# Pairwise bilinear products: two-tile x blocks, one PSUM ring, and some products moved to ACT and POOL

## The chip, the cores and the metric

The kernel runs on one core of one Trainium2 chip. The metric is the device time of that core in microseconds (us), the median of several executions. The engines are called PE (TensorE matmul), PEld (TensorE's loading of weights, which overlaps PE), DVE (VectorE), ACT (ScalarE), POOL (GpSimd) and SP (SyncE, which here only issues DMA transfers). All tensors are fp32.

## The reference, cut to what matters

```python
x: (4096, 32, 64)         # B samples, F fields, D
W: (496, 64, 64)          # one matrix for each pair i < j of fields
idx_i, idx_j = np.triu_indices(F, k=1)
vi = inputs[:, idx_i, :]
vj = inputs[:, idx_j, :]
vidots = jnp.einsum('bpd,pde->bpe', vi, W)
return vidots * vj        # (4096, 496, 64): 520 MB
```

The output is 520 MB, the inputs are 42 MB, and everything has to be moved once. At 432 GB/s, the best rate that the kernel before holds for a while, moving them takes 1303 us (an estimate).

## The kernel before

It takes x in 32 tiles of 128 samples, one per SBUF partition. TensorE turns pairs of fields so that the contracted dimension lies on the partitions. It multiplies field i by the matrices of its pairs, up to 16 pairs in one piece (46 pieces in a tile). VectorE multiplies each piece from PSUM by the fields x_j into an output buffer. Five groups of pieces make up a tile, and each group is stored by one DMA of about 3 MB from one of three buffers.

```python
    xpool = ctx.enter_context(tc.tile_pool(name="xpool", bufs=NX))          # NX = 3
    opool = ctx.enter_context(tc.tile_pool(name="opool", bufs=3))
    psum = ctx.enter_context(tc.tile_pool(name="psum", bufs=3, space=bass.MemoryType.PSUM))
    tpsum = ctx.enter_context(tc.tile_pool(name="tpsum", bufs=2, space=bass.MemoryType.PSUM))
    # ... cut ...
    def load_w(c: int):                       # four parts of w, one buffer
        a, b = wrows[c]
        raw[c] = rpool.tile([P, D * D], F32, tag="raw", name=f"raw_{c}")
        nc.sync.dma_start(out=raw[c][: b - a, :], in_=wflat[a:b])
    # ... cut: turn_w reorders a part, loads the next one, turns it into wT ...
    blocks = [(t, g) for g in range(len(groups)) for t in range(NX)]        # first three tiles group by group
    blocks += [(t, g) for t in range(NX, NT) for g in range(len(groups))]
    # ... cut: in the loop over all pieces ...
        nc.vector.tensor_mul(                 # every product, from PSUM
            ot[:, o : o + m, :].rearrange("p m (h e) -> p m h e", h=2),
            ps[:, :, :m, :].rearrange("p h m e -> p m h e"),
            xs[t][:, j + 1 : j + 1 + m, :].rearrange("p m (h e) -> p m h e", h=2),
        )
        if pa + m == end:
            nc.sync.dma_start(out=out[t * P : (t + 1) * P, base:end, :], in_=ot[:, : end - base, :])
            if g == len(groups) - 1 and t + NX < NT:
                load_x(t + NX, nc.scalar)
```

Of the kernel before, what the change touches and what calls it, by code (L numbers as in the profile page):

```python
# [8 lines left out]
F32 = mybir.dt.float32  # L9


@with_exitstack
def kernel(
    ctx: ExitStack,
    tc: tile.TileContext,
    x: bass.AP,
    w: bass.AP,
    out: bass.AP,
):








    nc = tc.nc

    B, F, D = x.shape  # L30
    P = 128
    assert 2 * D == P and B % P == 0
    NT = B // P
    NP = F * (F - 1) // 2
    E2 = D // 2
    BANK = 512
    CH = BANK // E2
    p0 = [i * (F - 1) - i * (i - 1) // 2 for i in range(F)]


    groups = [
        [(0, 3)],
        [(3, 5), (5, 7)],
        [(7, 9), (9, 11)],
        [(11, 14), (14, 17)],
        [(17, 20), (20, 23), (23, 26), (26, 29), (29, 31)],
    ]
    RUN = max(b - a for g in groups for a, b in g) + 1
    cap = max(p0[g[-1][1]] - p0[g[0][0]] for g in groups)

    cuts = [*range(0, NP, P), NP]
    wrows = list(zip(cuts[:-1], cuts[1:]))
    NX = 3

    const = ctx.enter_context(tc.tile_pool(name="const", bufs=1))
    rpool = ctx.enter_context(tc.tile_pool(name="rpool", bufs=1))
    ppool = ctx.enter_context(tc.tile_pool(name="ppool", bufs=2))
    xpool = ctx.enter_context(tc.tile_pool(name="xpool", bufs=NX))
    xtpool = ctx.enter_context(tc.tile_pool(name="xtpool", bufs=6))
    opool = ctx.enter_context(tc.tile_pool(name="opool", bufs=3))  # L60
    psum = ctx.enter_context(tc.tile_pool(name="psum", bufs=3, space=bass.MemoryType.PSUM))
    tpsum = ctx.enter_context(tc.tile_pool(name="tpsum", bufs=2, space=bass.MemoryType.PSUM))

    ident = const.tile([P, P], F32, tag="ident", name="ident")
    make_identity(nc, ident)

    xs = {}

    def load_x(t: int, eng):

        xs[t] = xpool.tile([P, F + 1, D], F32, tag="xs", name=f"xs_{t}")
        nc.gpsimd.memset(xs[t][:, 0, :], 0.0)  # L72
        eng.dma_start(out=xs[t][:, 1:, :], in_=x[t * P : (t + 1) * P])


    wflat = w.rearrange("p d e -> p (d e)")
    raw = {}
    wT = [
        const.tile([P, b - a, E2], F32, tag=f"w{c}", name=f"wT_{c}")
        for c, (a, b) in enumerate(wrows)  # L80
    ]
    EP = 8
    EU = BANK // P

    def load_w(c: int):
        a, b = wrows[c]
        raw[c] = rpool.tile([P, D * D], F32, tag="raw", name=f"raw_{c}")
        nc.sync.dma_start(out=raw[c][: b - a, :], in_=wflat[a:b])  # L88

    def turn_w(c: int, k: int, copy):  # L90
        r = wrows[c][1] - wrows[c][0]
        rp = ppool.tile([P, EP, 2, D], F32, tag="rp", name=f"rp_{c}_{k}")
        src = raw[c][:r, :].rearrange("p (d h e) -> p e h d", h=2, d=D)
        copy(rp[:r], src[:, k * EP : (k + 1) * EP])  # L94
        if k == E2 // EP - 1 and c + 1 < len(wrows):
            load_w(c + 1)
        for u in range(0, EP, EU):
            e0 = k * EP + u
            pt = tpsum.tile([P, EU, P], F32, tag="pt", name=f"ptw_{c}_{e0}")
            for n in range(EU):  # L100
                nc.tensor.transpose(  # L101
                    pt[:, n, :r],
                    rp[:r, u + n].rearrange("p h d -> p (h d)"),
                    ident[:r, :r],
                )
            nc.scalar.copy(  # L106
                wT[c][:, :, e0 : e0 + EU], pt[:, :, :r].rearrange("p e r -> p r e")
            )

    def turn_x(t: int, a: int, b: int):  # L110

        pt = tpsum.tile([P, RUN, P], F32, tag="pt", name=f"ptx_{t}_{a}")
        for n in range(b - a + 1):
            nc.tensor.transpose(  # L114
                pt[:, n, :],
                xs[t][:, a + n : a + n + 2, :].rearrange("p f d -> p (f d)"),
                ident,
            )
        xT = xtpool.tile([P, RUN, P], F32, tag="xT", name=f"xT_{t}_{a}")
        nc.scalar.copy(xT[:, : b - a + 1, :], pt[:, : b - a + 1, :])  # L120
        return xT

    load_x(0, nc.scalar)
    load_w(0)
    for t in range(1, NX):
        load_x(t, nc.sync)


    blocks = [(t, g) for g in range(len(groups)) for t in range(NX)]
    blocks += [(t, g) for t in range(NX, NT) for g in range(len(groups))]  # L130
    steps = [
        (t, g, r, i, c0, min(CH, F - 1 - i - c0))
        for t, g in blocks
        for r in groups[g]
        for i in range(*r)
        for c0 in range(0, F - 1 - i, CH)
    ]


    AHEAD = 6  # L140
    due: dict = {}
    seen = set()
    for s, (t, g, r, i, c0, m) in enumerate(steps):
        if (t, r) not in seen:
            seen.add((t, r))
            due.setdefault(max(0, s - AHEAD), []).append(("x", t, r))
        for c, (a, b) in enumerate(wrows):
            if c and a < p0[i] + c0 + m and c not in seen:
                seen.add(c)
                for k in range(E2 // EP):  # L150
                    due.setdefault(s - 18 + 4 * k, []).append(("w", c, k))

    engines = [nc.vector.tensor_copy, nc.gpsimd.tensor_copy, nc.scalar.copy, nc.vector.tensor_copy]
    for k in range(E2 // EP):
        turn_w(0, k, engines[k])

    xT = {}
    ot = None
    for s, (t, g, r, i, c0, m) in enumerate(steps):
        for what, *args in due.get(s, ()):  # L160
            if what == "x":
                tt, rr = args
                xT[tt, rr] = turn_x(tt, *rr)
            else:
                turn_w(*args, nc.gpsimd.tensor_copy)

        base, end = p0[groups[g][0][0]], p0[groups[g][-1][1]]
        pa = p0[i] + c0
        if pa == base:
            ot = opool.tile([P, cap, D], F32, tag="ot", name=f"ot_{t}_{g}")  # L170
        ps = psum.tile([P, 2, CH, E2], F32, tag="ps", name=f"ps_{s}")
        for c, (a, b) in enumerate(wrows):
            lo, hi = max(pa, a), min(pa + m, b)
            if lo < hi:
                for h in range(2):
                    rows = slice(h * D, (h + 1) * D)
                    nc.tensor.matmul(  # L177
                        ps[:, h, lo - pa : hi - pa, :],
                        xT[t, r][rows, i - r[0] + 1 - h, :],
                        wT[c][rows, lo - a : hi - a, :],  # L180
                        start=True,
                        stop=True,
                    )
        o = pa - base
        j = i + 1 + c0
        nc.vector.tensor_mul(  # L186
            ot[:, o : o + m, :].rearrange("p m (h e) -> p m h e", h=2),
            ps[:, :, :m, :].rearrange("p h m e -> p m h e"),
            xs[t][:, j + 1 : j + 1 + m, :].rearrange("p m (h e) -> p m h e", h=2),
        )  # L190
        if pa + m == end:
            nc.sync.dma_start(
                out=out[t * P : (t + 1) * P, base:end, :],
                in_=ot[:, : end - base, :],
            )
            if g == len(groups) - 1 and t + NX < NT:
                load_x(t + NX, nc.scalar)


# [25 lines left out]
```

## Time and profile before

| | before |
|---|---|
| median of 3 runs | 1371.99 us (1371.41 to 1372.5) |
| bytes moved | 562.97 MB |
| one tile in the middle | 41.4 us |
| first store issued | 35.48 us |

The head of the profile page gives the span and, for each engine, the busy time, its share of the span and the number of instructions. The fourth part gives the chain of work that ended last, as shares of the span by engine.

```profile
span 1370.6 us, 18821 instructions
...
PE 1292.4 (94%) x7776; PEld 675.2 (49%) x7776; DVE 1183.4 (86%) x1474; ACT 227.5 (17%) x418; POOL 31.4 (2%) x51
...
PE 50%; DMA 32%; DVE 16%; issue 1%; POOL 0%; DVEq 0%; POOLq 0%; SPq 0%
```

The chain runs through PE for half of the span, and PE is busy for 94% of it.

### The profile page before, as it was taken

To read this page: it belongs to the slowest core of one execution; us is meant where nothing else is said; L and a number is where in the kernel's file an instruction comes from. 1 tells how busy PE (TensorE), PEld (TensorE's weight loads), DVE (VectorE), ACT (ScalarE), POOL (GpSimd) and SP (SyncE) were. 2 spreads that over 40 slices of the span, in tenths; PEclk is the share of its full clock that TensorE was granted. 3 is DMA by queue.
4 is the path that set the end of the run, shared out by engine and by line. 5 is a ranking of instruction groups with operands and counts; after the bars stand their busy time and mean duration, and the time that the engine had idled before them with its cause. 6 is when DMAs were issued, how large, how long until landed. Compare 5 with 4: busy or idle time off the path is not lost.

```text
span 1370.6 us, 18821 instructions
## 1 busy us (share of the span) xinstructions
PE 1292.4 (94%) x7776; PEld 675.2 (49%) x7776; DVE 1183.4 (86%) x1474; ACT 227.5 (17%) x418; POOL 31.4 (2%) x51
## 2 busy tenths in 40 slices
PE   5999999999999999999999999999999999999995
PEld 3555554444554445544445554455544445544553
DVE  2888899888889888989889889899898889898995
ACT  2222211111111111111111111111111111111110
POOL 2220000000000000000000000000000000000000
PEclk9999999999999999999999999999999999999998
DMA  5999999999999999999999999999999999999998
GB/s 214 382 406 405 410 430 432 431 424 419 410 422 428 414 416 421 414 425 419 415 421 414 419 425 423 416 397 426 424 423 418 410 416 418 422 427 417 421 404 354
DMA packets 28292, 562.97 MB, mean 411 GB/s; under 512 B 3136, under 2 KB 3136, under 8 KB 3136
## 3 DMA queue, kind: packets, MB, share of 16 engines
q1 hardware_dynamic: 23888, 530.33, 91.8%
q10 hardware_dynamic: 4320, 31.46, 5.5%
q8 instruction: 61, 1.00, 0.3%
q14 instruction: 23, 0.19, 0.0%
HBM read 41.68 MB, written 520.09 MB: 410 GB/s over the span
## 4 chain that ended last, share of the span: by engine, by line
PE 50%; DMA 32%; DVE 16%; issue 1%; POOL 0%; DVEq 0%; POOLq 0%; SPq 0%
PE ps L177 38%; DMA out_dram<-ot 31%; DVE ot L186 16%; PE ptx L114 10%; DMA raw<-in_L_rec_W_dram 1%; PE ptw L101 1%; DVE rp L94 0%; POOL rp L94 0%; DVEq L186 0%; POOLq L94 0%; SPq L88 0%; DVEq L94 0%
## 5 line engine op out<-in xcount | busy, mean ns | idle before, releaser
L186 DVE TENSOR_TENSOR ot<-ps,xs 128x1024 f32<-128x1024 f32 (+7 forms) x1472 | 1181.3, 868 | 157.7 <-PE ps L177 99.8
L177 PE MATMUL ps<-wT,xT 64*128 64x512 f32 (+13 forms) x6272 | 1090.8, 467 | 46.9 <-DVE ot L186 44.5
L177 PEld LDWEIGHTS ps<-wT,xT 64*128 64x128 f32 x6272 | 515.4, 186 | 509.3 <-DVE ot L186 302.0
L120 ACT COPY xT<-ptx 128x512 f32<-128x512 f32 (+1 forms) x384 | 207.5, 541 | 1088.7 <-PE ptx L114 1086.3
L114 PE MATMUL ptx<-ident,xs 128*128 128x128 f32 x1376 | 240.9, 290 | 0.2 <-ACT wT L106 0.2
L114 PEld LDWEIGHTS ptx<-ident,xs 128*128 128x128 f32 x1376 | 144.5, 141 | 145.6 <-issue 138.5
L101 PE MATMUL ptw<-ident,rp 128*128 128x128 f32 (+1 forms) x128 | 20.5, 304 | 16.6 <-DVE rp L94 12.5
L72 POOL MEMSET xs<- 128x64 f32 x32 | 4.8, 151 | 1130.5 <-DVE ot L186 1090.8
L101 PEld LDWEIGHTS ptw<-ident,rp 128*128 128x128 f32 (+1 forms) x128 | 15.6, 156 | 26.0 <-issue 16.1
L94 POOL COPY rp<-raw 128x1024 f32<-128x1024 f32 (+1 forms) x13 | 26.0, 2018 | 74.0 <-DMA raw<-in_L_rec_W_dram 32.1
L106 ACT COPY wT<-ptw 128x512 f32<-128x512 f32 (+1 forms) x32 | 17.4, 574 | 35.7 <-PE ptw L101 35.7
L94 DVE COPY rp<-raw 128x1024 f32<-128x1024 f32 x2 | 2.1, 1026 | 15.4 <-DMA raw<-in_L_rec_W_dram 11.4
L94 ACT COPY rp<-raw 128x1024 f32<-128x1024 f32 x1 | 1.9, 1945 | 0.0
L106 ACT ACT_TABLE_LOAD x1 | 1.3, 1283 | 1.2 <-PEq L212 1.2
masks.py:199 POOL TENSOR_SCALAR_AFFINE_SELECT ident<-ident 128x128 f32<-128x128 f32 x1 | 0.3, 292 | 0.0
masks.py:197 POOL MEMSET ident<- 128x128 f32 x1 | 0.2, 204 | 0.3 <-POOLq L212 0.3
L212 POOL MEMSET const-float32-0.0<- 128x1 f32 x1 | 0.1, 99 | 0.2 <-issue 0.2
L212 POOL MEMSET const-bfloat16-1.0<- 128x1 bf16 x1 | 0.1, 102 | 0.0
L212 POOL MEMSET const-uint8-127<- 128x1 uint8 x1 | 0.1, 102 | 0.0
L212 POOL MEMSET const-float32-1.0<- 128x1 f32 x1 | 0.1, 99 | 0.0
## 6 DMA issues: line engine op xcount, KB each, us to landing
out_dram<-ot SPq DMA_DIRECT2D x64, 3360.0 KB, 15.5
out_dram<-ot SPq DMA_DIRECT2D x64, 2880.0 KB, 15.7
out_dram<-ot SPq DMA_DIRECT2D x32, 3392.0 KB, 16.8
xs<-in_r_inputs_dram ACTq DMA_DIRECT2D x30, 1024.0 KB, 14.5
raw<-in_L_rec_W_dram SPq DMA_DIRECT2D x3, 2048.0 KB, 10.6
xs<-in_r_inputs_dram SPq DMA_DIRECT2D x2, 1024.0 KB, 13.6
raw<-in_L_rec_W_dram SPq DMA_DIRECT2D x1, 1792.0 KB, 10.4
```

The source lines that it names most:

```text
L72: nc.gpsimd.memset(xs[t][:, 0, :], 0.0)
L94: copy(rp[:r], src[:, k * EP : (k + 1) * EP])
L101: nc.tensor.transpose(pt[:, n, :r], rp[:r, u + n].rearrange("p h d -> p (h d)"), ident[:r, :r],)
L106: nc.scalar.copy(wT[c][:, :, e0 : e0 + EU], pt[:, :, :r].rearrange("p e r -> p r e"))
L114: nc.tensor.transpose(pt[:, n, :], xs[t][:, a + n : a + n + 2, :].rearrange("p f d -> p (f d)"), ident,)
L120: nc.scalar.copy(xT[:, : b - a + 1, :], pt[:, : b - a + 1, :])
L177: nc.tensor.matmul(ps[:, h, lo - pa : hi - pa, :], xT[t, r][rows, i - r[0] + 1 - h, :], wT[c][rows, lo - a : hi - a, :], start=True, stop= ...
L186: nc.vector.tensor_mul(ot[:, o : o + m, :].rearrange("p m (h e) -> p m h e", h=2), ps[:, :, :m, :].rearrange("p h m e -> p m h e"), xs[t][ ...
L212: nc = _bacc.Bacc("TRN2", target_bir_lowering=False, num_devices=1)
```

## The change

The intent is to free the compute engines, so that the DMA alone sets the pace, and to start the output earlier. x comes in blocks of two tiles by one load. Eight fields are turned at once into one 1024-element PSUM tile. One PSUM ring of four serves everything. Seven of the 46 products of a tile go through an ACT copy and a POOL multiplication. The parts of w are loaded at once into buffers that are not needed yet.

```diff
+    NB = 2
-    psum = ctx.enter_context(tc.tile_pool(name="psum", bufs=3, space=bass.MemoryType.PSUM))
-    tpsum = ctx.enter_context(tc.tile_pool(name="tpsum", bufs=2, space=bass.MemoryType.PSUM))
+    psum = ctx.enter_context(tc.tile_pool(name="psum", bufs=4, space=bass.MemoryType.PSUM))
+    aside = (1, 3, 5, 7, 9, 11, 13)
 ... cut: x loads of 2 tiles, "(p k) f d -> p (k f) d" ...
-        raw[c] = rpool.tile([P, D * D], F32, tag="raw", name=f"raw_{c}")
+        pool, tag = ((opool, "ot"), (xpool, "xs"), (const, "w3"), (xpool, "xs"))[c]
+        raw[c] = pool.tile([P, D * D], F32, tag=tag, name=f"raw_{c}")
 ... cut: turn_x of RUN = 8 fields; all 4 parts of w turned within the first tile ...
+    load_w(0)
+    load_w(1)
+    load_x(0, nc.sync, 1, NB)
+    load_w(2)
 ... cut ...
+        if i in aside and c0 == 0:
+            tmp = tpool.tile([P, CH, 2, E2], F32, tag="tmp", name=f"tmp_{s}")
+            nc.scalar.copy(tmp, src)
+            nc.gpsimd.tensor_mul(dst, tmp, xj)
+        else:
+            nc.vector.tensor_mul(dst, src, xj)
-                out=out[t * P : (t + 1) * P, base:end, :],
+                out=rows_of(out, blk).rearrange("(p k) n d -> p k n d", k=NB)[:, kt, base:end, :],
```

The order also changes. The kernel before made the first three tiles group by group, so it needed each part of w late. The changed one goes tile by tile from the start.

## The prediction

> **What bounds the kernel now.** I began with the page's slices, which show each engine and the DMA over forty equal stretches (34.3 us each):
>
> ```profile
> PE   5999999999999999999999999999999999999995
> DVE  2888899888889888989889889899898889898995
> DMA  5999999999999999999999999999999999999998
> GB/s 214 382 406 405 410 430 432 431 424 419 410 422 428 414 416 421 414 425 419 415 421 414 419 425 423 416 397 426 424 423 418 410 416 418 422 427 417 421 404 354
> DMA packets 28292, 562.97 MB, mean 411 GB/s; under 512 B 3136, under 2 KB 3136, under 8 KB 3136
> ```
>
> Three things are near full at once: TensorE, VectorE and the DMA. "9" does not tell a full pipe from a nearly full one, but the last row does: slices six to eight reach 430 to 432 GB/s, and later ones mostly 414 to 425. So the pipe has a few per cent left in the long middle, and half of the first slice is empty. I then asked for stretches (columns: stretch, length, busy us of PE, PEld, DVE, ACT, POOL, granted clock, DMA share, GB/s):
>
> ```profile
> 160.00:200.00 40.00, 39.56 (x244) 20.70 (x243) 36.87 (x46) 6.49 (x12) 0.15 (x1) 1.00 1.01 433
> 242.42:283.80 41.38, 39.64 (x241) 20.43 (x239) 36.87 (x46) 6.49 (x12) 0.15 (x1) 1.00 1.01 431
> 325.20:366.60 41.40, 39.09 (x233) 20.57 (x230) 36.83 (x45) 6.01 (x11) 0.00 (x0) 0.96 0.98 412
> 1030.32:1071.71 41.39, 39.61 (x241) 20.42 (x239) 36.88 (x46) 6.49 (x12) 0.15 (x1) 1.00 0.99 418
> 0.00:41.40 41.40, 24.37 (x110) 14.83 (x112) 12.20 (x12) 11.80 (x18) 11.40 (x14) 0.92 0.59 231
> ```
>
> One tile of 128 rows takes 41.39 us in the middle and asks for 17.3 MB (16.25 written, 1.05 read): 418 GB/s. At the 432 GB/s that the same kernel holds for 100 us while a backlog of output is queued, 17.3 MB need 40.05 us. The compute side thus sets the 41.39 us, with TensorE busy for 39.6 of it, and the DMA is only 1.3 us behind. The waits show how the three hand over (engine, what it waited for, total us, times, longest):
>
> ```profile
> PEld ps L177 <- DVE ot L186: 302.0, 594, 2.7
> ...
> DVE ot L186 <- PE ps L177: 99.8, 150, 5.5
> DVE ot L186 <- DMA out_dram<-ot: 50.1, 48, 2.3
> PE ps L177 <- DVE ot L186: 44.5, 86, 1.8
> ```
>
> VectorE waits now for products, now for a free output buffer; TensorE waits for a PSUM slot. No single engine is the bound. The start is different (time order: start, length, engine, operation):
>
> ```profile
> 25.85 3.77 POOL L94 COPY rp<-raw 128x1024 f32<-128x1024 f32 x2 [11.67 <-DMA raw<-in_L_rec_W_dram]
> ...
> 35.48 0.35 SPq L192 DMA_DIRECT2D out_dram<-ot  x1
> ```
>
> The single raw buffer makes w's second part load late; POOL reorders it at 25.85 us, TensorE's queue stands behind it, and the first output is issued only at 35.48. The trace's packets show the pipe empty from about 15 to 18.5 and 25 to 36.5 us.
>
> **The skill against this trace.** "DMA: Bandwidth & Descriptors", section "Where 436 GB/s comes from", puts the fabric's ceiling at 435 GB/s. The trace agrees: a 23,040-byte output packet takes 855 ns in the median, 26.9 GB/s on each of 16 engines, 431 together. The same page's 358 GB/s per core is not seen here: 411 is the mean. "GPSIMD Engine Reference", section 3.1, gives 4497 ns for a two-input fp32 operation on 2048 elements; half, about 2.25 us, is my estimate for a 1024-element product. The trace has only POOL copies (2.0 us for 1024), which fits. "SBUF — State Buffer", section "Who interferes with whom", says that a VectorE instruction with one SBUF input does not contend with GpSimd. A product reads PSUM and SBUF, so I expect none; the trace has too little POOL work to show it. "TensorE: Matmul & The Clock Gate", section on HAM oscillation, warns of idle gaps over about 3.4 us. Two dips to half clock of 3.4 us each, at 344 and 883 us, are in the clock record; the stretch above with 0.96 holds the first, and its DMA fell to 412.
>
> **The change, part by part, per tile of 128 rows.** Durations are from these groups (line, engine, operation, tiles, count, total us, mean ns of one):
>
> ```profile
> L186 DVE TENSOR_TENSOR ot<-ps,xs 128x1024 f32<-128x1024 f32 x512 | 623.5, 1218 | 132.7 <-PE ps L177 81.8 <-DMA out_dram<-ot 50.1
> ...
> L114 PE MATMUL ptx<-ident,xs 128*128 128x128 f32 x1376 | 240.9, 290 | 0.2 <-ACT wT L106 0.2
> ...
> L120 ACT COPY xT<-ptx 128x512 f32<-128x512 f32 x224 | 131.0, 585 | 618.8 <-PE ptx L114 616.4 <-PE ps L177 2.4
> ...
> L120 ACT COPY xT<-ptx 128x384 f32<-128x384 f32 x160 | 76.5, 478 | 469.9 <-PE ptx L114 469.9
> ```
>
> *Turning x:* 1376/32 = 43 transposes become 32. In time order four take 0.66 us, 0.165 each, so TensorE saves 11 x 0.165 = 1.8 us. Twelve ACT copies (6.5 us) become four of 1024 elements. The two sizes above give 0.84 ns an element plus 155 ns, so 1.01 us each, 4.0 in all.
>
> *Products moved:* seven of 1024 elements leave VectorE. Its six products in a row for the first group (5760 elements) took 6.49 us, so one of 1024 is 1.15: VectorE goes from 36.9 to about 28.8 us. ACT gets 7 x 1.01 = 7.1, in all 11. POOL gets 7 x 2.25 = 16. Both are far below 40, and no moved product is the last of its output group.
>
> *One PSUM ring of four:* TensorE may run one step further ahead, so some of the 302 + 44 us of waiting for VectorE (10.8 per tile, overlapping) goes. TensorE at 39.6 - 1.8 = 37.8 us, less what its modelled ends contain of waiting, no longer needs 40.
>
> *Loads and stores:* bytes are unchanged. The x packets become 16 KB in place of 8 KB, which at 7 ns a packet (from 309 ns for 8,192 and 611 for 16,384 bytes) is under 1 us in total. Outputs keep their packet sizes but go to every second row.
>
> So after the start the DMA alone sets the pace: about 40.1 to 40.3 us per tile instead of 41.39.
>
> *The start:* x's first half and three of w's four parts (8.4 MB with x's second half) are queued at once and keep the pipe full until about 22 us: 19.4 us of data plus 2 to 3 us of slow first packets, as w's first ones show (1.2 to 1.5 us instead of 0.61). w's first part still lands near 11.4 us, and four pieces turned take the first matmul to about 19 (21.5 before). The first group needs 90/496 of about 30 us of matmuls, 5.4, and three w turns at 1.15, then one product: issue near 30, data from 31.5. That leaves some 9 us empty, against about 15. But all of w is now turned within one tile, not three: TensorE has about 48 us of work there, and I count 4 us more of gaps and slow w reads before it stops mattering.
>
> *The sum.* 562.97 MB at 432 GB/s are 1303 us. Add 2 before the first byte, 3 slow first reads, 9 empty before the first output, 4 in the rest of the first tile, 3 for slow w reads beside output (those packets averaged 790 to 940 ns), 4 for small losses over 31 tiles, and 4.4 between the last packets and the end (1366.2 to 1370.6 before) plus 1 in the drain: 1333. The timed median is 1.4 us above the profiled span: about 1335. I put the point a little higher because the surprises are on that side: 1337.
>
> **Rivals.** (1) *Reads and writes disturb each other.* w's 16 KB packets beside output took up to 940 ns where 611 is clean. The x packets now have that size; if all 2048 lost 190 ns, 2048 x 190/16 = 24 us come back and the time is about 1358. Against it: in the backlogged stretches the 8 KB x packets cost nothing (432 GB/s with the x load in it), and they alternate with output on another queue, as these will. (2) *The compute side stays the bound:* ACT stands in the PSUM ring twice, for turns and moved products, and each x load makes it wait for POOL's memset. If a tile still took 41 us, the gain would be the start alone, about 8 us: 1364. Against it: the largest engine sum is 37.8. (3) *Clock dips:* TensorE will idle more while it waits for the DMA, so half-clock windows may come more often. One such window costs about 1.7 us of a tile with some 3 to 5 us of slack and two queued outputs, so I give it under 5 us: 1340. (4) *The row stride of the stores doubles to 248 KiB* and HBM might serve it worse; nothing in the trace speaks to it, and 3% slower packets would undo everything, 1372.
>
> **Range and chances.** The floor of this plan is near 1325: nothing lost after the start. Rivals 1 and 2 in part reach 1358. The 2% line is 1344.6 us, 8 above my point. I give 0.70 for faster, 0.29 within, 0.01 slower.
>
> **What would show it.** Right: middle slices at 429 to 433 GB/s; VectorE near 29 us a tile and waiting mostly for the output DMA; first output issued near 30 us. Wrong: x or output packets longer than 611 and 855 ns in the median (rivals 1, 4); GB/s near 418 with TensorE waiting for ACT (rival 2); the first output not earlier than 35 us.

## The result, and the profile after

| | before | after |
|---|---|---|
| median, same rounds | 1371.70 us (1370.6 to 1372.5) | 1359.86 us (1359.48 to 1364.98) |
| profiled span | 1370.6 | 1357.5 |
| first store issued | 35.48 | 29.97 |

The ratio is 0.9923, with a 95% interval of 0.9898 to 0.9947. A ratio is the mean time of one kernel's fast runs over that of the other's fast runs of the same rounds, so it is not quite the ratio of the medians. The kernel became 0.8% faster, which is inside the 2% that counts as the same. The predicted 1337 us was 23 us too low, and the measured time lies just above 1358, up to which the prediction's range reached. Its likeliest outcome, faster by more than 2% (0.70), did not come.

The same slices of the page for the changed kernel, each now 33.9 us long (PEclk is the granted TensorE clock in tenths):

```profile
PE   5998988888888888988889888899888889888894
...
DVE  5686876767677676766667767677776777767783
...
PEclk9998998989999999998989999999898999999997
DMA  7999999999999999999999999999999999999997
GB/s 291 388 430 431 426 424 431 431 422 426 401 424 413 430 423 412 428 409 431 410 417 425 413 433 407 421 423 410 428 412 424 426 409 424 406 431 428 417 419 335
```

VectorE has fallen to 6 or 7 tenths, and TensorE has holes. Only the DMA row is full. Yet the GB/s row is half of what the prediction named as a sign of being wrong: near 418. The other half, TensorE waiting for ACT, did not come (3.2 us in all). In slices three to nine the flow lies between 422 and 431, and from there on it swings between 401 and 433. A freed compute side did not raise the flow. The groups (line, engine, operation, tiles, count, total us, mean ns of one, idle time before them) confirm the durations:

```profile
L209 DVE TENSOR_TENSOR ot<-ps,xs 128x1024 f32<-128x1024 f32 (+15 forms) x1248 | 938.6, 807 | 378.4 <-DMA out_dram<-ot 195.3
...
L207 POOL TENSOR_TENSOR ot<-tmp,xs 128x1024 f32<-128x1024 f32 x224 | 527.3, 2360 | 623.5 <-ACT tmp L206 397.7
L206 ACT COPY tmp<-ps 128x1024 f32<-128x1024 f32 x224 | 226.7, 1012 | 465.5 <-PE ps L192 460.6
```

That mean of 807 ns mixes shapes; the 1024-element products alone are this group:

```profile
L209 DVE TENSOR_TENSOR ot<-ps,xs 128x1024 f32<-128x1024 f32 x288 | 351.1, 1219 | 80.4 <-PE ps L192 79.6
```

The waits (engine, what it waited for, total us, times, longest):

```profile
DVE ot L209 <- DMA out_dram<-ot: 195.3, 97, 5.2
POOL ot L207 <- DMA out_dram<-ot: 169.5, 73, 5.6
DVE ot L209 <- PE ps L192: 156.9, 212, 2.7
```

VectorE's wait for a free output buffer was 50.1 us before, and it is 195.3 us now. The compute side is ahead and waits for the DMA, as the change intended. The chain agrees, where the DMA had 32% before and PE 50%:

```profile
DMA 50%; PE 23%; DVE 18%; POOL 4%; issue 3%; ACT 0%; DVEq 0%; SPq 0%; POOLq 0%; ACTq 0%
```

The time line shows when x is loaded, once every two tiles, and so the pace (start, length, engine):

```profile
602.75 0.34 ACTq L75 DMA_DIRECT2D xs<-in_r_inputs_dram  x1
685.94 0.34 ACTq L75 DMA_DIRECT2D xs<-in_r_inputs_dram  x1
767.97 0.34 ACTq L75 DMA_DIRECT2D xs<-in_r_inputs_dram  x1
```

Two tiles took 83.19 and 82.03 us, a mean of 41.3 us per tile. **The pace of the steady part hardly changed**: by the packet records used below, two tiles took 82.94 us before and 82.72 after. Nearly all of the gain lies in the first 170 us. In the first 41.4 us the kernel now moves 300 GB/s, where it moved 231:

```profile
0.00:41.40 41.40, 27.47 (x168) 17.86 (x168) 22.18 (x20) 15.25 (x15) 18.72 (x15) 1.00 0.76 300
```

In slices one to five the kernel before is 333 GB/s below 430 in sum (214, 382, 406, 405, 410); at 34.3 us a slice and 430 GB/s that is 26.5 us of transfers not made. The changed one is 184 below (291, 388, 430, 431, 426), which is 14.5 us. The difference is 12 of the 13 us by which the span fell.

**What holds the DMA at 41.4 us.** The printed views average over sixteen DMA engines. I therefore went to the records of single packets in the trace, of which no view exists; the numbers from here to the end of the section are my own sums of them. A packet without disturbance takes 855 ns (23,040 bytes), 996 (26,880), 1006 (27,136) or 611 (16,384, x). Each engine moves eight packets of each store, so two tiles without disturbance are 2 x 8 x (0.855 + 1.006 + 0.855 + 0.996 + 0.996) + 8 x 0.611 = 80.2 us, with the small completion packets 80.3. That is 40.15 us per tile, close to the prediction's 40.05.

But the sixteen engines do not finish a store together. In the steady part fifteen end within 1 to 2 us of each other, and one ends 5 to 6 us after their median. I followed that last engine packet by packet over 15 of the 16 stores of four tiles (each engine's eight data packets, the completion packet and those of x). Each packet starts when the one before it ends: the gap is zero within the 0.02 us of a store that the records resolve. It is never idle, and its packets are longer: 879 ns in the mean instead of 855, 1029 instead of 996, 1046 instead of 1006. Two tiles take it 82.7 us. Followed further, from 305 to 1341 us, it stays the same engine through 127 stores with 0.5 us of gaps in all. Of its output packets there 5% are undisturbed; of the other fifteen engines' it is 66%. There are three output buffers and a store frees its buffer only when its last packet has landed, so the fifteen others soon wait for this one.

The lag of the last engine behind the median of the others, read at the second store of a tile, shows when this begins. It is 1.7 us at 98 us, 2.8 at 180, 4.4 at 263 and 6.5 at 346 us, and it stays between 4.7 and 6 from there. While the lag grows, the core shows 422 to 431 GB/s. When the buffers are used up, all engines go at the pace of the slowest. The kernel before does the same (1.2 us at 190 us, 5.1 at 356, then 3.5 to 5.1). Its lagging engine is hardly ever idle either: from 562 to 985 us, through 52 stores, its gaps are 0.1 us in all.

### The profile page after: what moved, and what is told of

Its sections match the earlier page's. It is cut to its first block, busy times and chain, and to the rows that moved or that the text cites. A ratio compares the mean times of both kernels' runs of the same rounds, so it can differ in the third digit from the quotient of the medians.

```text
span 1357.5 us, 17867 instructions
## 1 busy us (share of the span) xinstructions
PE 1171.5 (86%) x7424; PEld 681.2 (50%) x7424; DVE 951.3 (70%) x1259; ACT 371.1 (27%) x367; POOL 546.2 (40%) x253
## 4 chain that ended last, share of the span: by engine, by line
DMA 50%; PE 23%; DVE 18%; POOL 4%; issue 3%; ACT 0%; DVEq 0%; SPq 0%; POOLq 0%; ACTq 0%
DMA out_dram<-ot 49%; PE ps L192 19%; DVE ot L209 18%; PE ptx L113 4%; POOL ot L207 3%; DMA raw<-in_L_rec_W_dram 1%; POOL rp L94 1%; PE ptw L103 0%; ACT tmp L206 0%; DVE rp L94 0%; DVEq L209 0%; DVE xT L117 0%; ACT wT L106 0%; SPq L211 0%; POOLq L207 0%
## 5 line engine op out<-in xcount | busy, mean ns | idle before, releaser
L209 DVE TENSOR_TENSOR ot<-ps,xs 128x1024 f32<-128x1024 f32 (+15 forms) x1248 | 938.6, 807 | 378.4 <-DMA out_dram<-ot 195.3
L192 PE MATMUL ps<-wT,xT 64*128 64x512 f32 (+14 forms) x6272 | 1025.2, 467 | 118.0 <-DVE ot L209 105.5
L192 PEld LDWEIGHTS ps<-wT,xT 64*128 64x128 f32 x6272 | 554.0, 193 | 554.6 <-DVE ot L209 281.9
L207 POOL TENSOR_TENSOR ot<-tmp,xs 128x1024 f32<-128x1024 f32 x224 | 527.3, 2360 | 623.5 <-ACT tmp L206 397.7
L206 ACT COPY tmp<-ps 128x1024 f32<-128x1024 f32 x224 | 226.7, 1012 | 465.5 <-PE ps L192 460.6
L117 ACT COPY xT<-ptx 128x1024 f32<-128x1024 f32 x127 | 128.5, 1012 | 470.2 <-PE ptx L113 470.2
L113 PE MATMUL ptx<-ident,xs 128*128 128x128 f32 x1024 | 143.8, 285 | 48.9 <-DVE ot L209 34.3
L113 PEld LDWEIGHTS ptx<-ident,xs 128*128 128x128 f32 x1024 | 113.2, 144 | 95.4 <-issue 51.3
L106 ACT COPY wT<-ptw 128x1024 f32<-128x1024 f32 (+1 forms) x15 | 14.7, 984 | 28.1 <-PE ptw L103 28.1
L94 DVE COPY rp<-raw 128x1024 f32<-128x1024 f32 (+1 forms) x9 | 11.0, 1233 | 12.3 <-DMA raw<-in_L_rec_W_dram 11.9
```

The costliest lines, as they stand in the source:

```text
L94: copy(rp[:r], src[:, k * EU : (k + 1) * EU])
L106: copy(wT[c][:, :, k * EU : (k + 1) * EU], pt[:, :, :r].rearrange("p e r -> p r e"))
L113: nc.tensor.transpose(pt[:, n, :], xs[blk][:, s : s + 2, :].rearrange("p f d -> p (f d)"), ident)
L117: copy(xT, pt)
L192: nc.tensor.matmul(ps[:, h, lo - pa : hi - pa, :], xT[blk, kt, n // RUN][h * D : (h + 1) * D, n % RUN, :], wT[c][h * D : (h + 1) * D, lo - ...
L206: nc.scalar.copy(tmp, src)
```

## The experiments

Fourteen kernels ran, all in three timed rounds and, where nothing else is said, with correct results. "Two tiles" is the time from one store of the lagging engine to the same store two tiles on, averaged over ten such pairs (tiles 6 to 26), again my own reading of packet records. Square brackets after a time hold the 95% interval of its ratio to the kernel before. "A" in the expectations is the theory that TensorE's instruction stream stretches the packets of the lagging engine; up to halves and onepass it has the form that this engine also fetches TensorE's instructions. "B" is a rival that differs from run to run.

| kernel | PE and PEld instructions | two tiles, us | median, us | ratio to before |
|---|---|---|---|---|
| no_pe (wrong) | 0 | 81.05 | 1323.12 | 0.9652 |
| best | 8,576 | 81.78 | 1348.95 | 0.9843 |
| onepass | 8,576 | 81.84 | 1347.39 | 0.9826 |
| all_dve | 14,848 | 82.66 | 1357.49 | 0.9903 |
| after | 14,848 | 82.72 | 1359.86 | 0.9923 |
| thin_pe (wrong) | 14,848 | 82.74 | 1360.36 | 0.9924 |
| before | 15,552 | 82.94 | 1371.70 | 1 |
| halves | 22,272 | 83.73 | 1380.45 | 1.0058 |
| pool_tied | 14,848, and 5,888 more on POOL | 84.15 | 1379.55 | 1.0069 |

### Does the compute side or the DMA hold the pace: no_pe and thin_pe

no_pe takes all of TensorE's work away, and ACT's and POOL's part of the products with it. It keeps every load and store, through three fixed output buffers; its outputs are wrong.

```diff
-                        nc.tensor.matmul( ... )      # and all transposes
+        nc.vector.tensor_mul(dst[:, :1], xj[:, :1], xj[:, :1])
```

> Wrong result on purpose: the changed kernel's loads and stores, all 160 of the same size and order through the same three output buffers, but no TensorE work and one small VectorE product per step. Theory A (one DMA engine is the bound, because it also carries TensorE's instruction blocks of 16 KB, 58 of them at about 0.65 us, which is 38 us): without TensorE's instructions no engine lags, and the time is about 1318 us, with middle slices at 430 to 434 GB/s. Rival B (the compute chain through PSUM, half-clock windows and three buffers sets the pace): about 1318 us too. Rival C (stores to every second row, or stores at all, can't be served faster than now): about 1350 us.

thin_pe keeps all of TensorE's work but lets VectorE multiply only one pair of each piece, and ACT and POOL none; its outputs are wrong too. (Both cuts leave out the fixed buffers.)

```diff
-        if i in aside and c0 == 0:
-            ... ACT copy, POOL product ...
-        else:
-            nc.vector.tensor_mul(dst, src, xj)
+        nc.vector.tensor_mul(dst[:, :1], src[:, :1], xj[:, :1])
```

> Wrong result on purpose: the changed kernel with its whole TensorE stream, the turns, and the same loads and stores, but each product writes one pair in place of up to 16, so VectorE, ACT and POOL have little to do. Theory A: TensorE's instruction blocks are all there, so the time stays within 6 us of the changed kernel, 1352 to 1364 us, and one DMA engine ends several us after the other fifteen. Rival B: with VectorE nearly free TensorE needs under 36 us a tile, the compute chain is out of the way, and the time falls to 1318 to 1330 us.

no_pe took 1323.12 us [ratio 0.9638 to 0.9666] and thin_pe 1360.36 [0.9909 to 0.9939]. First the busy row and the GB/s row of no_pe, then the busy row of thin_pe:

```profile
DVE 242.8 (18%) x1484; POOL 24.8 (2%) x29
...
GB/s 373 416 430 434 434 426 434 427 433 430 426 430 428 431 431 428 432 427 431 431 426 434 424 432 429 428 431 429 431 428 431 432 423 431 426 435 428 433 434 310
```

```profile
PE 1143.2 (84%) x7424; PEld 706.0 (52%) x7424; DVE 324.0 (24%) x1485; ACT 144.6 (11%) x143; POOL 27.7 (2%) x30
```

no_pe holds 423 to 435 GB/s from the third slice to the last but one, so the same transfers can go nearly at the predicted pace. Its expectation missed one thing: an engine lags here too, by up to 8.1 us at the end. But it lags in another way: 96% of its output packets are undisturbed, and a few are very long (25 of 853, from 291 to 1156 us, by more than 12%). thin_pe has VectorE at 24%, so it cannot be late, and it still needs 41.4 us per tile. That takes VectorE, ACT and POOL off the list: with TensorE's stream in the program the pace is 41.4, without it 40.5. no_pe alone could not show this, as both of its theories expected the same time. The pair does not yet tell TensorE's duration (84% busy) from its instructions.

### Whether one engine's share of the bytes can be lightened: split120

Every fourth tile's first group was stored as 120 and 8 partitions.

```diff
+            for a0, b0 in (((0, 120), (120, P)) if g == 0 and t % 4 == 2 else ((0, P),)):
+                nc.sync.dma_start(out=dst_rows[a0:b0, kt, base:end, :], in_=ot[a0:b0, : end - base, :])
```

> Right result: in every fourth tile the first output group is stored in two parts, partitions 0 to 119 and 120 to 127. If a store of 120 rows runs on the 15 lowest DMA engines and one of 8 rows on the 8 lowest, the highest engine is relieved of 8 x 8 packets of 855 ns, 55 us, and the lowest eight get 8 x 0.86, 7 us. Theory A if the lagging engine is the highest one: 1325 to 1335 us. Theory A if it is one of the lowest eight: about 7 us longer, 1366. If it is in between: no change, 1358 to 1361. Rival B: no change or slightly longer.

It took 1437.85 us (1410 to 1457), and its profile fell in the slow state. Its two fast runs, 1429 and 1410 us, already make it slower than the kernel before, by 3.6% [1.0275 to 1.0438]. The issue lines (KB of each, us from issue to landing) of the slow profile show where to look:

```profile
out_dram<-ot SPq DMA_DIRECT2D x64, 3360.0 KB, 15.2
...
out_dram<-ot SPq DMA_DIRECT2D x8, 2700.0 KB, 31.6
```

A store of 120 partitions takes twice as long as a larger one of 128, and 566 of the 1,024 packets of 23,040 bytes in the split groups took more than 1.5 us instead of 0.855. Why splitting makes packets slow is not shown, and no fast profile of it exists. The question of which engine lags stays open; nothing in the records names an engine.

### Are the moved products worth anything: all_dve

```diff
-    aside = (1, 3, 5, 7, 9, 11, 13)
+    aside = ()
```

> Right result: the changed kernel with no product moved to ACT and POOL, so VectorE has all 46 per tile, some 36.9 us, again. Theory A: the pace of 41.3 us a tile is not VectorE's, so within 4 us of the changed kernel. Rival B: VectorE and TensorE wait for each other more, and at least half of the 12 us gained is lost: 1366 us or more.

It took 1357.49 us [0.9889 to 0.9918], 2.4 us less than the changed kernel. VectorE is back at 88%, and the pace does not change (82.66 us for two tiles):

```profile
PE 1189.6 (88%) x7424; PEld 674.8 (50%) x7424; DVE 1189.2 (88%) x1483; ACT 144.6 (11%) x143; POOL 17.7 (1%) x29
```

The moved products, the largest part of the change, earn nothing, because VectorE was not what the kernel waited for.

### More and fewer TensorE instructions: halves and onepass

halves issues each matmul of more than eight pairs as two. It has the same columns and results, and half as many TensorE instructions again.

```diff
+                    mid = lo + 8 if hi - lo > 8 else hi
+                    for u0, u1 in ((lo, mid), (mid, hi)):
+                        if u0 < u1:
                             nc.tensor.matmul( ... u0, u1 ... )
```

> Right result: the changed kernel with every matmul of more than eight pairs issued as two. The same columns go through TensorE, but its program grows from 14,887 to 22,311 instructions, from 58 to 87 blocks of 16 KB. Theory A (one DMA engine carries these blocks besides its sixteenth of the data and sets the pace): 29 blocks at about 0.65 us more, so 1358 + 19 = 1377 us, give or take 5. Rival B (the compute chain): TensorE has some 4 us of slack a tile, so 1358 to 1364 us.

onepass declares the turned x and w as float32r, so that each product takes one matmul in the trace and not two (3,136 in place of 6,272). The data type is not exact fp32, which a user must be free to accept; the outputs passed the comparison with the reference.

```diff
-        xT = xtpool.tile([P, RUN, P], F32, tag="xT", ...)
+        xT = xtpool.tile([P, RUN, P], mybir.dt.float32r, tag="xT", ...)
-            wT[c] = const.tile([P, r, E2], F32, tag=f"w{c}", ...)
+            wT[c] = const.tile([P, r, E2], mybir.dt.float32r, tag=f"w{c}", ...)
```

> Products in the one-pass form of fp32 (operands rounded by the copies that write them), so the result may miss the tolerance; that is not the point. TensorE's program shrinks from 14,887 to 8,615 instructions, from 58 to 33.7 blocks, and the matmuls take less time. Theory A: 24.5 blocks less at 0.65 us, 1343 us, give or take 5. Rival B: TensorE is far from busy and the compute chain is gone: 1320 to 1330 us.

halves took 1380.45 us [1.0034 to 1.0082], inside the expected 1377 give or take 5. (Its profile is of the fastest run, 1374.98 us; the other three took 1380.4 to 1381.0, and why is not known.) onepass took 1347.39 [0.9809 to 0.9842], also close to A. That A's numbers came true does not show its fetching; what speaks against that stands under "What stays open". The busy row of halves, then the busy and clock rows of onepass:

```profile
PE 1206.3 (88%) x11136; PEld 1081.3 (79%) x11136; DVE 953.2 (69%) x1259; ACT 371.3 (27%) x367; POOL 546.1 (40%) x253
```

```profile
PE 960.1 (71%) x4288; PEld 630.4 (47%) x4288; DVE 946.7 (70%) x1259; ACT 370.8 (28%) x367; POOL 548.8 (41%) x253
...
PEclk9755555555555555555655555565555555555555
```

halves hardly changes PE's busy time (88% against 86%), and PE still waits; onepass runs at half the granted clock for nearly all of the time and is faster. So neither TensorE's busy time nor its clock is what counts. The time follows the number of instructions. (What grows along with it, the weight loads' time for one, 681 to 1081 us in halves, these two runs don't separate.) Between onepass, after and halves two tiles rise by 0.88 us for 6,272 instructions and by 1.01 us for 7,424: 0.140 and 0.136 us per thousand, a straight line. no_pe lies 0.4 us above that line carried to zero (82.72 - 14.848 x 0.138 = 80.67). The lagging engine's own packets show the same order. Those of 23,040 bytes take 874 ns in the mean in onepass (468 to 729 us), 883 in the changed kernel, 892 in halves and 900 in pool_tied, the last experiment below, and in none of the stretches that could be followed (260 to 1035 us long) is that engine idle for more than 0.7 us in all.

### Smaller stores: fine

Nine groups and five output buffers in place of five and three. If a late engine only costs at the end of each store, more and smaller buffers help.

```diff
-    groups = [(0, 3), (3, 7), (7, 11), (11, 17), (17, F - 1)]
+    groups = [(0, 2), (2, 4), (4, 6), (6, 8), (8, 11), (11, 14), (14, 18), (18, 23), (23, F - 1)]
-    opool = ... bufs=3
+    opool = ... bufs=5
```

> Right result: nine output groups per tile with five buffers in place of five with three, in the same space. Theory A: the lagging engine stays as busy as before and only the first store comes earlier, so 1352 to 1359 us. Rival B (three buffers too few to cover a slow group): the stores never run dry and the time falls to 1325 to 1340 us.

It took 1370.87 us [0.9975 to 1.0019], slower than the changed kernel: rival B falls, and A's number missed as well. A tile took 41.63 us, by packets. Four more stores of eight packets per engine at 7 ns each (the constant part of the packet times) are 0.22 us a tile, or 7 us in all. That is an estimate which accounts for most of the miss; I did not test it apart.

### The start: late_w and late_w2

late_w loads w's later parts only when the part before has been reordered, as before the change.

```diff
     load_w(0)
-    load_w(1)
     load_x(0, nc.sync, 1, NB)
-    load_w(2)
+    # load_w(1) after the last order_w(0, .), load_w(c + 1) after the last turn_w(c, .)
```

> Right result: the changed kernel with w's parts loaded one after the other again, each when the one before has been reordered. Theory A says that all of the gain of 12 us lies before the stream of stores is full, so most of it goes: 1366 to 1373 us. If the gain came from the steady part, 1358 to 1362.

It took 1361.63 us [0.9915 to 0.9944], which lies in the second range but tells little. The loads of the second and third parts were issued within the first 3 us all the same. Their buffers were free, and SyncE issues a load as soon as nothing that it has to wait for stands before it. The edit thus changed almost nothing. late_w2 has the same order of loads and puts the first three parts through one buffer, which makes the loads serial.

```diff
-        pool, tag = ((opool, "ot"), (xpool, "xs"), (const, "w3"), (xpool, "xs"))[c]
+        pool, tag = ((const, "w3"), (const, "w3"), (const, "w3"), (xpool, "xs"))[c]
```

> The changed kernel with w's four parts loaded one after the other through one buffer (the fourth through x's), each when the part before has been reordered, as in the kernel before; late_w did not make them serial. If the gain of 12 us is the start (first store 5.5 us earlier, and fewer holes in the traffic before the stream of stores is full): most of it goes, 1364 to 1371, with an unchanged pace of 41.4 us per tile afterwards. If early w loads earn nothing because only the time of the first store counts: 1358 to 1363.

It took 1385.59 us [1.0095 to 1.0126], 26 us more than the changed kernel, at an unchanged pace of 82.73 us for two tiles. The direction was right and the size far off. The time line of SyncE's queue (start, length, operation) shows why:

```profile
1.64 16.55 SPq L88 DMA_DIRECT2D raw<-in_L_rec_W_dram  x2
40.36 0.35 SPq L211 DMA_DIRECT2D out_dram<-ot  x1
40.80 0.38 SPq L88 DMA_DIRECT2D raw<-in_L_rec_W_dram  x1
66.30 56.64 SPq L211 DMA_DIRECT2D out_dram<-ot  x8
```

The first store is issued at 40.36 us, and the second waits until 66.30, since the first tile needs all of w. The kernel before hid its late loads behind the first group of three tiles. The new order of tiles and the early loads therefore belong together: the start's gain is a net of two large terms, and the early loads are worth 26 us to this order.

### Both helpful edits: best and best2

best is all_dve with the float32r of onepass.

> All products on VectorE (2.4 us better than the changed kernel) together with one-pass fp32 in TensorE (12.5 us better). If the two act on different things: 1359.9 - 2.4 - 12.5 = 1345. If what all_dve gained was the same thing (fewer instructions and waits in all): 1347, as onepass alone. Expected 1345, range 1343 to 1348, so 1.9% faster than the kernel before. Not exact fp32: products are rounded more, the outputs must still agree with the reference.

It took 1348.95 us [0.9828 to 0.9858], no better than onepass alone. Its pace was a little better (81.78), but its first store's packets began at 30.5 us where onepass's began at 27.0. I took this for VectorE's doing, as it makes the first tile alone there, and best2 gives the helpers back in the first tile only:

```diff
-        if i in aside and c0 == 0:
+        if i in aside and c0 == 0 and t == 0:
```

> onepass, with ACT and POOL helping in the first tile only. best missed its 1345: its pace was 40.88 us per tile (onepass 40.91) but its first store began 3.5 us later (30.5 instead of 27.0), by our reading since VectorE alone makes the first tile. If that reading is right: onepass's start and best's pace, 1347.4 - 0.03*31 = 1346.5 (1345.5 to 1347.5). If the helpers were worth more than the start, 1347.5 to 1349.

It took 1348.59 us (1346.87 to 1349.72) [0.9830 to 0.9862]. In its profile the first store began at 27.1 us and the span was 1345.1, against 1346.8 for best and 1345.5 for onepass. The start moved as expected, but the timed runs do not separate the three. The reading of the cause was also too quick. In best the first store was issued only 0.9 us later than in onepass (27.11 instead of 26.19 us). But the fourth part of w was issued at 23.0 us, before it, and its packets held the queue until 30.5 and beyond, where onepass and best2 issue it just after the store. So most of the delay was that load's. onepass, best and best2 all beat both kernels by more than their intervals, by 0.8 to 1.0% against the changed one (the ratio of their ratios, as they ran in other rounds) and by 1.5 to 1.7% against the one before, at the price of exact fp32.

### Any engine's instructions, or TensorE's alone: pool_instr, pool_paced, pool_tied

all_dve with four tiny POOL instructions after each of the 1,472 pieces.

```diff
+        for n in range(4):
+            nc.gpsimd.memset(dot[:, n : n + 1], 0.0)
```

> The changed kernel with all 46 products on VectorE, and four one-column memsets by POOL after each of the 1,472 pieces: 5,888 more instructions on an engine that is otherwise idle; TensorE, VectorE and the transfers as in all_dve (1357.5 us). Theory A1, any engine's instruction stream stretches the packets of the lagging DMA engine: from halves and no_pe some 0.060 us per tile and thousand instructions, so 0.35 us per tile and 1357.5 + 11 = 1368.5 (1365 to 1372). Theory A2, TensorE's stream alone does (by its place, or because it has two instructions, weight load and matmul, for each step): 1355 to 1360. Rival C, POOL's work slows VectorE[...]: shows as longer tensor_mul durations than in all_dve.

It took 1414.53 us [1.0305 to 1.0340] and settled nothing. The memsets depend on nothing, so POOL ran them all in the first 270 us, ahead of its share of turning w. The steady part, without them, was as in all_dve (82.67 us for two tiles). pool_paced made one of the four wait for the piece.

```diff
+        nc.gpsimd.tensor_copy(dot[:, 0:1], ot[:, o, 0:1])
+        for n in range(1, 4):
+            nc.gpsimd.memset(dot[:, n : n + 1], 0.0)
```

> pool_instr ran all its memsets in the first 250 us, ahead of POOL's share of the start, so it said nothing of the pace. Here POOL's four one-column instructions per piece follow VectorE's product of that piece (the first copies one column of it), so 184 of them run in each tile, 5,888 in all; else as all_dve (1357.5 us, 41.32 us per tile). Theory A1, any engine's instructions count: slope 0.060 us per tile and thousand instructions from no_pe and halves, so 41.32 + 0.35 = 41.68 us per tile and 1357.5 + 11 = 1369 (1365 to 1373). Theory A2, TensorE's alone count: 41.3 to 41.4 us per tile and 1356 to 1361. If VectorE's products get longer or POOL becomes late (releasers of the stores), the run decides nothing.

It took 1489.10 us [1.0851 to 1.0888], for the same reason: the three memsets still ran ahead. One copy per piece was left in the steady part, and two tiles took 83.20 us instead of 82.66. So pool_tied lets the memsets write the copy's column, which keeps their order.

```diff
+        nc.gpsimd.tensor_copy(dot[:, 0:1], ot[:, o, 0:1])
+        for n in range(3):
+            nc.gpsimd.memset(dot[:, 0:1], 0.0)
```

> In pool_paced the memsets ran ahead again, and only one small copy per piece (92 in two tiles) was left for the steady part, where two tiles took 83.10 us instead of all_dve's 82.57. Here the three memsets write the same column as the copy, so all four follow the product: 368 POOL instructions in two tiles. What costs: by the bytes of their fetch (pool_paced's 5,888 more instructions added 57 blocks of 8 KB, so 3.6 more blocks in two tiles, 309 ns each at the pace of a clean 8 KB packet): 83.7 us in two tiles and 1357.5 + 18 = 1375; by the number of instructions at TensorE's slope (0.12 us in two tiles and thousand of the program): 83.3 and 1369; by what each tied POOL instruction cost in pool_paced (0.53 us for 92): 84.7 and 1391; nothing, if POOL's instructions don't count: 82.6 and 1357.5.

It took 1379.55 us [1.0054 to 1.0084], 22 us more than all_dve. The start was as in all_dve (first store at 32.3 us against 32.8), and two tiles took 84.15 us, 1.49 more, for 368 more POOL instructions. The slices of POOL and the GB/s row:

```profile
POOL 4654555545455454554545555455554545545553
...
GB/s 319 390 427 431 434 418 421 397 425 416 401 411 403 432 412 411 409 404 421 410 421 412 404 417 416 413 405 409 421 396 425 417 403 412 410 423 411 418 413 321
```

POOL's instructions are now spread evenly, and the flow falls from the seventh slice on. VectorE's products kept their 869 ns, so this is not a slower VectorE. The cost is 4.0 ns per POOL instruction. TensorE's slope in the same unit is 2.2 ns: 0.138 us in two tiles for a thousand of the program, of which a sixteenth (62) falls in two tiles. The expectation by bytes of instructions (83.7 us, 1375) came nearest and was too low. So TensorE is not special: instructions of an engine that is otherwise idle cost the lagging DMA engine time as well. The lagging engine's chain has no gap of more than 0.03 us from 307 to 1280 us, so this is not a wait for POOL. One limit remains: the copies wait for VectorE's product and all four follow one another, and the run does not separate that from their being fetched.

## Why the prediction was wrong

**The step that failed** is this one: "So after the start the DMA alone sets the pace: about 40.1 to 40.3 us per tile instead of 41.39." Its first half held, its figure did not. The DMA alone does set the pace, but at 41.36 us, and it had set it before too, at 41.47. "The compute side thus sets the 41.39 us" was wrong. The 40.05 us came from "the 432 GB/s that the same kernel holds for 100 us while a backlog of output is queued". Those 100 us were a transient: fifteen engines running ahead of the sixteenth until the three output buffers were used up.

**The mis-sized term** of the sum is "4 for small losses over 31 tiles". What stands in its place is the stretch of the lagging engine: 82.72 - 80.3 = 2.4 us in two tiles, some 37 us over 31. The sum with measured terms closes. Undisturbed packets give 1307 us for each engine (the median time of each size, with the completion and instruction packets that the prediction's 1303 leaves out). What undisturbed packets do not fill of the first 41.4 us is 12.7 us (the prediction's 2, 3 and 9 make 14). With the 37 this is 1357, against a last packet at 1356. The separate terms for the rest of the first tile and for slow w reads, 7 us, are then not needed. Nor was the term of 4.4 us "between the last packets and the end" what it was taken for. In the kernel before, fifteen engines had ended by 1366.3 us, and the last one's data ended at 1369.05. That was the lagging engine, in plain sight before the prediction was made.

**"No single engine is the bound"** was wrong of the kernel before, since one DMA engine was. The mean over sixteen engines, 418 GB/s, hid it. VectorE waited only 50 us for the DMA, most likely because TensorE and VectorE took just about as long as the lagging engine. When they were freed, the wait grew to 195 us and the time per tile stayed.

**The start was right, and better than predicted.** Of the 35 us that the prediction hoped for, the 12 that came are the start's, for which it had counted about 8. The first matmul began at 20.03 us (19 predicted), and the first store was issued at 29.97 ("near 30"). One reading was loose: the parts of w that came beside output before took 789 and 898 ns a packet in the mean (some over 1400), not "790 to 940". **The durations were right:** a POOL product took 2360 ns (2.25 us predicted), a 1024-element ACT copy 1012 ns (1.01), and VectorE was busy for 951.3 / 32 = 29.7 us a tile (28.8). The Trainium skill's "GPSIMD Engine Reference" was a good source for POOL. The expected absence of contention between VectorE and POOL also held: a 1024-element product took 1219 ns after and 1218 before. Since VectorE was not the bound, none of this bought time.

**The rivals.** Rival 1 (slow x packets) fell: their median is 611 ns. Rival 4 (the row stride) fell: output packets kept their 855, 996 and 1006 ns. That rival 1 had named nearly the right time (1358) is luck. Rival 2 came near too (1364), for a wrong cause, as all_dve and thin_pe show. Rival 3 (the clock) was common and harmless: there are 21 half-clock windows of 3.4 or 6.8 us, and onepass is faster with the clock at half for nearly all of its time. A fifth rival was missing: that sixteen engines which share one store need not finish together.

**What stays open.** Shown are that the lagging engine is hardly ever idle in the followed stores, that its packets are stretched, and that the stretch grows in a line with TensorE's instructions and also with POOL's. Not shown is how. The Trainium skill, "Runtime: NRT & Kernel Launch", section "Instruction fetch mechanics", says that instructions come by DMA in blocks of 16 KiB, 256 each, at a cost that is "mostly hidden". The count fits: 14,848 / 256 = 58 blocks, and the page of the changed kernel has this line:

```profile
q8 instruction: 58, 0.95, 0.3%
```

The size does not rule it out. 58 / 16 blocks in two tiles are 2.2 us at the 611 ns of an undisturbed packet of that size, and 3.4 us at the 935 ns that they took in the median, if all of them fell on one engine; the stretch is 2.4. These products are estimates. The placing speaks against it. None of the 45 blocks between 305 and 1341 us lies among the lagging engine's packets, and those are stretched nearly all by a little, only two of 1,011 output packets by more than 12%. So fetching on that very engine is not the way there, and how instructions slow it stays open. One rival was not tested: each timed run has a span and a granted clock, so a profiler was recording in all of them, and a cost of recording each instruction would look the same.

## What to carry to other kernels

Before calling a stream of stores "almost bound by the DMA", look at when each engine finishes a store and not only at the mean rate, and do not take the rate of the first 300 us for the lasting one: here, with three buffers, the slowest DMA engine set the pace only after its lag had used them up. Test the bound by emptying an engine (thin_pe, no_pe) before moving work off it. When the DMA is full, fewer instructions may be worth more than shorter ones: here a thousand TensorE instructions cost 2 to 3 us (onepass, the changed kernel and halves).

## What the Trainium skill lacked or had wrong

- "Runtime: NRT & Kernel Launch", section "Instruction fetch mechanics", calls the cost of fetching "mostly hidden". In this kernel, whose DMA is full, time follows the number of TensorE instructions: 1347 us with 8,576, 1360 with 14,848 and 1380 with 22,272. Whether fetching is the way is not shown, and on the lagging engine itself none was found from 305 to 1341 us, so this does not prove the page wrong.
- "DMA: Bandwidth & Descriptors", section "Latency and other measured facts", says that two of the sixteen engines are usually slower and, as a best guess, puts it down to descriptors made in software. Here the data go by hardware queues alone, and still one engine ends 5 to 6 us after the median of the others, and its packets are 24 to 40 ns longer. Whether it is one of those two the records don't say.
- The same page's ceiling of 435 GB/s is reached by no_pe in a single slice (435, with 430 typical); the lasting rate with TensorE at work was about 418 (17.3 MB in 41.36 us). No page that I read says that instructions of the compute engines lower the rate of a full DMA.
- "TensorE: Matmul & The Clock Gate", section on HAM oscillation, warns of the half clock and gives no case in which it is harmless. It came 21 times here within the run, and onepass ran at it nearly throughout (mean granted clock 0.526) and was 12.5 us faster.
